# Stationary operands in one piece, two orders of tokens, a column of ones for the denominators, and new schedule constants, in a fused graph-attention and slice-attention layer

## The chip, the cores and the metric

The kernel runs on one core of one Trainium2 chip. The time is device microseconds (us) from launch to end, and a run is one execution. All runs in this document were in the fast state. A profile shows one execution; its engines are PE (TensorE matmuls), PEld (TensorE weight loads, which overlap PE: they are busy for 79% of the span of the kernel before, beside 97% of PE), DVE (VectorE), ACT (ScalarE), POOL (GpSimd) and SP (SyncE, which issues the transfers here).

## The reference, cut to what matters

The input is 32 independent graphs ("batches" below) of 512 tokens with 256 features, all fp32.

```python
x = x + gnn(layernorm(x), adj)        # x: [32, 512, 256]
x = x + ffn(layernorm(x))

def gnn(x, adj):
    out = relu(x @ mlp1_w + mlp1_b)                      # 256 -> 512
    out = elu(gat(out, None, W_fc, a_fc)) + out          # attention over all tokens
    out = relu(out @ mlp2_w + mlp2_b)                    # 512 -> 256
    return relu(elu(gat(out, adj, W_hand, a_hand)) + out)    # masked attention

def gat(inp, mask, W, a):
    h = inp @ W
    e = leaky_relu((h @ a1)[:, :, None] + (h @ a2)[:, None, :])   # masked where adj == 0
    return elu(softmax(e, axis=2) @ h)

def ffn(x):      # 8 heads; the 512 tokens are pooled into 64 slice tokens per head
    w = softmax((x_mid @ W_slice) / temp)                # 512 x 64 weights per head
    token = (w.T @ fx_mid) / (w.sum() + 1e-5)
    token = attention(token)                             # 64 x 64 per head
    return (w @ token) @ W_out
```

## The kernel before

The kernel records all operations of the 32 batches first. A greedy scheduler with a cost model then decides the order of instructions on every engine, and they are issued in that order. The constants that steer it (`TURNS`, `PERIOD`, and shifts `HEAD`, `TAIL` of the first and last three batches) appear to have been tuned for this kernel (b_new_turns below shows another set doing worse in it). The scheduler sees the tiles that each operation reads and writes, its modelled cost, and a key (the time at which its step should have its turn):

```python
TURNS = {"load": -28.1, "norm1": 42.5, "mlp1": 51.4, "h": 105.5, ...}   # key of each step
PERIOD, SPARE = 91.4, 0.00
HEAD, TAIL = (-48.2, -40.6, -1.9), (-3.9, 8.3, 26.1)
...
    def order(self):
        ...                                    # a first schedule of 12 batches gives starts
        shift = dict(enumerate(HEAD)) | {last - i: s for i, s in enumerate(reversed(TAIL))}
        ...
        keys[op] = (age - SAMPLE) * period + turn + shift.get(age, 0.0)
        ...
        return self._schedule(self.ops, keys.get, SPARE)     # greedy, lowest key first

    def emit(self):
        for op in self.order():
            getattr(getattr(self.nc, op.engine), op.method)(*op.args, **op.kwargs)
```

A batch's 512 tokens are loaded so that partition p holds tokens 4p to 4p+3; block t (t = 0..3, `NT` = 4) has token 4p+t at partition p. Where a product needs the features on the partitions, the tile is transposed: VectorE transposes blocks of 32 by 32 into a stage, and five transfers through DRAM move the blocks to their places. For the first and last batch TensorE transposes instead.

```python
    def flip(src, dst):
        nc.vector.transpose(dst, src.rearrange("p (c i) -> p c i", i=Q))     # Q = 32

    def gather(what, stage, dst):
        scr = dram.tile(...)
        for a in range(P // Q):
            nc.sync.dma_start(scr[:, :, a, :].rearrange("c r j -> r c j"), stage[ts(a, Q), :, :])
        nc.sync.dma_start(dst, scr.rearrange("(k c) r a j -> (c r) k (a j)", c=P // Q))

    def every(cols, t):
        return cols[:, t::NT]                  # a step of four words
```

The stage is written with a step (`flip(e, stage[:, :, i::NT])`), so that the columns of the transposed tile are the tokens in natural order. A product whose result shall have block t on its partitions then takes its stationary operand with a step of four words. `matmul(out, stationary, moving)`:

```python
        nc.step = "h"                                     # first attention, W_fc
        ...         nc.tensor.matmul(pm, every(o0T[:, k], t), wfc[:, k, s, :], ...)
        nc.step = "mlp2"
        ...         nc.tensor.matmul(pm, w2[:, k, ts(m)], o1T[:, k, :], ...)
        nc.step = "e"                                     # masked attention
            nc.scalar.activation(e, e, AF.Exp, bias=nmax[:, i:i+1], accum_out=den[:, i:i+1])
            flip(e, stage[:, :, i::NT])
        gather("e", stage, pT)
        nc.vector.reciprocal(rd, den)
        nc.step = "pv2"
        ...         nc.tensor.matmul(pm[:, s, :], every(pT[:, j], i), h[:, j, :D], ...)
        nc.step = "w"                                     # slice weights
        ...         nc.tensor.matmul(pm, every(xnT[:, k], t), weff[:, k, :], ...)
                    flip(wt, stage[:, :, t::NT])
        gather("w", stage, wT)
        nc.step = "tokens"
        ...         nc.tensor.matmul(pm[ts(s, C), p, :], wfx[:, k, ts(2 * p + s, C)],
                                     every(s1T[:, k], p)[:, ts(s, G)], ...)       # 64 wide
        for s in range(2):
            nc.tensor.matmul(pm[ts(s, C)], bfx[:, ts(s, C)], nrow[:, s], ...)     # bias
        nc.step = "out"
        ...         nc.tensor.matmul(po[:, s, :], every(wT[:, p], t), gg[:, p, :], ...)
```

In the groups of the profile these are `mm<-wfc,o0T` (h), `mm<-o1T,w` (mlp2), `mm<-h,p2T` (pv2), `mm<-weff,xn2T` (w), `mm<-xn,w` (sums), `mm<-s1T,wfx` and `mm<-nrow,bfx` (tokens), and `mm<-gg,wT` (out). Every instruction passes through the scheduler's `emit`, so all of them carry the same line number.

Of the kernel before, what the change touches and what calls it, by code (L numbers as in the profile page):

```python
# [16 lines left out]
    "load": -28.1, "norm1": 42.5, "mlp1": 51.4, "h": 105.5, "factors": 105.5, "p": 114.2,  # L17
    "pv": 115.4, "o1": 126.5, "mlp2": 169.7, "h2": 183.7, "e": 190.4, "p2": 190.4,
    "pv2": 203.8, "norm2": 210.0, "w": 285.7, "sums": 288.2, "s1T": 298.5, "tokens": 342.3,
    "att": 351.0, "vo": 351.0, "gg": 361.3, "out": 377.9,  # L20
}
PERIOD, SPARE = 91.4, 0.00

HEAD, TAIL = (-48.2, -40.6, -1.9), (-3.9, 8.3, 26.1)
# [6 lines left out]
P = 128  # L31
# [4 lines left out]
class Recorder:  # L36
# [5 lines left out]
    ISSUE, BEGIN, LAND, BEHIND = 0.45, 1.2, 0.9, 3.0  # L42
# [63 lines left out]
    def _cost(self, op, out, ins):  # L106
# [6 lines left out]
        if op.method == "dma_start":  # L113
            side = next(ap for ap in (out, *ins) if ap.space != bass.MemoryType.DRAM)
            op.moving = out.size() * 4 / (250e3 if side.ap[0][1] <= P // 4 else 320e3)
            return self.ISSUE, 0.0
# [175 lines left out]
def adj_ffn_kernel(  # L292
# [71 lines left out]
    def gather(what, stage, dst):  # L364


        blocks, width = stage.shape[1:]
# [9 lines left out]
    def every(cols, t):  # L377

        return cols[:, t::NT]
# [100 lines left out]
    nc.sync.dma_start(adjt, adj.rearrange("(p t) j -> p t j", p=P))  # L480
    for t in range(NT):
        nc.vector.tensor_scalar(
            mbias[:, t, :].rearrange("p (t q) -> p t q", t=NT),
            adjt[:, t, :].rearrange("p (q t) -> p t q", t=NT), 0.0, None, op0=OP.is_gt,
# [96 lines left out]
    def transpose_features(what, b, src, dst):  # L581

        if by_dma(what, b):
            stage = new(what + "_stage", [P, D // Q, P], tag="stage4")
            for t in range(NT):
                flip(src[:, t, :D], stage[:, :, t::NT])
            gather(what, stage, dst)
            return
        for k in range(KD):
            pt = tr_tile([P, N])  # L590
            for t in range(NT):
                nc.tensor.transpose(pt[:, ts(t)], src[:, t, ts(k)], ident)
            nc.scalar.copy(
                dst[:, k, :].rearrange("p (q t) -> p t q", t=NT),
                pt.rearrange("p (t q) -> p t q", t=NT),
            )
# [13 lines left out]
    def front(b):  # L610
# [8 lines left out]
        transpose_features("xn", b, xn, xnT)  # L619
# [13 lines left out]
        for t in range(NT):  # L633
            for s in range(2):
                pm = mm_tile([P, HH + 1])
                for k in range(KH):
                    nc.tensor.matmul(
                        pm, every(o0T[:, k], t), wfc[:, k, s, :],
                        start=(k == 0), stop=(k == KH - 1),
                    )  # L640
# [48 lines left out]
        for i in range(NT):  # L689
# [11 lines left out]
            if by_dma("u", b):  # L701
                flip(u, stage[:, :, i::NT])
# [4 lines left out]
            nc.vector.tensor_tensor(o1T[:, :, i::NT], pt, o0T[:, :, i::NT], op=OP.add)  # L707
        nc.step = "o1"
        if by_dma("u", b):
            gather("u", stage, o1T)  # L710
            for m in range(KH):
                nc.vector.tensor_tensor(o1T[:, m, :], o1T[:, m, :], o0T[:, m, :], op=OP.add)
        return o1T

    def middle(b, o1T):
# [3 lines left out]
        for m in range(KD):  # L719
            pm = mm_tile([P, N])  # L720
            for k in range(KH):
                nc.tensor.matmul(
                    pm, w2[:, k, ts(m)], o1T[:, k, :], start=(k == 0), stop=(k == KH - 1)
# [4 lines left out]
        for t in range(NT):  # L728
            pm = mm_tile([P, D + 2])
            for k in range(KD):  # L730
                nc.tensor.matmul(
                    pm, every(o2T[:, k], t), wh[:, k, :], start=(k == 0), stop=(k == KD - 1)
# [11 lines left out]
        den = small("den", [P, NT])  # L744
        nmax = small("nmax", [P, NT])
        for i in range(NT):
# [8 lines left out]
            nc.scalar.activation(  # L755
                e, e, AF.Exp, bias=nmax[:, i : i + 1], accum_out=den[:, i : i + 1]
            )
            if by_dma("e", b):
                flip(e, stage[:, :, i::NT])
# [4 lines left out]
            nc.scalar.copy(pT[:, :, i::NT], pt)  # L764
# [3 lines left out]
        rd = small("rd2", [P, NT])  # L768
        nc.vector.reciprocal(rd, den)

        r2 = new("r2", [P, NT, D])
        if by_dma("o2", b):
            stage = new("o2_stage", [P, N // Q, KD * Q], tag="stage4")
            for k in range(KD):
                nc.vector.transpose(
                    stage[:, :, ts(k, Q)].rearrange("p (t c) i -> p t c i", t=NT),
                    o2T[:, k, :].rearrange("p (c i t) -> p t c i", t=NT, i=Q),
                )
            gather("o2", stage, r2)
        else:  # L780
            for t in range(NT):
                pt = tr_tile([P, D])
# [263 lines left out]
```

## Time and profile before

| | before |
|---|---|
| time, median of the first 3 runs | 2926.81 us (2921.08 to 2928.37) |
| profiled span, granted TensorE clock | 2918.5 us, 0.991 |
| TensorE busy | 97% |
| weight loads busy | 79% |
| VectorE busy | 76% |
| ScalarE busy | 36% |

One number does most of the work below. The **period** is the time from the first mlp2 matmul of the 7th batch to that of the 27th, over 20: what one batch costs in the steady middle. It was 87.87 us. The **ends** are the span less 32 periods: filling, draining, and whatever batches near the two ends cost above or below the period. They were 2918.5 - 32 x 87.87 = 106.7 us. The span is then a sum of two things that different parts of the change may move. The prediction shows the views of the kernel before on which it rests.

### The profile page before, as it was taken

How to read it: one execution, taken by the hardware profiler on the slowest of the kernel's cores; microseconds unless marked ns; L12 is line 12 of the kernel's file. 1: busy time of each engine (PE TensorE's matmuls, PEld its weight loads, DVE VectorE, ACT ScalarE, POOL GpSimd, SP SyncE). 2: the span in 40 equal slices, each digit the busy share in tenths (PEclk: the TensorE clock that was granted, in tenths of full speed). 3: DMA queues.
4: the chain of work that ended last, by engine and by line, in shares of the span. 5: the costliest groups of instructions: out<-in, count | busy, mean ns of one | idle time of the engine just before them, and what ended most of it. 6: DMA issues, size and time to landing. Idle time of an engine off the chain costs nothing.

```text
span 2918.5 us, 34260 instructions
## 1 busy us (share of the span) xinstructions
PE 2827.3 (97%) x11981; PEld 2301.0 (79%) x11981; DVE 2231.4 (76%) x4994; ACT 1042.8 (36%) x2058; POOL 125.2 (4%) x233
## 2 busy tenths in 40 slices
PE   8999899999999999999999999999999999999998
PEld 6787668887778887878887878887878877777776
DVE  6567768877778877778877778877778877788774
ACT  3533323333333333333333333333333333333232
POOL 0000000000000000000000000000000000000000
PEclk9999999999999999999999999999999999999998
DMA  5125345454445454445444445444445444444420
GB/s 163 31 72 143 96 128 152 129 147 131 134 139 151 127 148 129 135 135 157 123 145 130 137 137 156 126 144 130 138 137 153 129 140 129 136 138 116 137 73 15
DMA packets 459365, 373.24 MB, mean 128 GB/s; under 512 B 82229, under 2 KB 376761, under 8 KB 459065
## 3 DMA queue, kind: packets, MB, share of 16 engines
q1 hardware_dynamic: 455856, 368.92, 43.8%
q10 hardware_dynamic: 3336, 2.14, 0.2%
q8 instruction: 95, 1.56, 0.2%
q14 instruction: 78, 0.63, 0.1%
HBM read 196.91 MB, written 174.06 MB: 127 GB/s over the span
## 4 chain that ended last, share of the span: by engine, by line
PE 61%; DVE 21%; DMA 11%; SPq 3%; issue 2%; ACT 1%; DVEq 0%; ACTq 0%
PE mm L255 58%; DMA scr<-e_stage 5%; DVE e_stage L255 4%; SPq L255 3%; DMA o1T<-scr 3%; DVE e L255 3%; DVE w L255 3%; DVE w_stage L255 2%; PE tr L255 2%; DVE rs L255 2%; DVE nmax L255 2%; DMA scr<-u_stage 1%; PE sm L255 1%; DVE u L255 1%; DVE mx L255 1%
## 5 line engine op out<-in xcount | busy, mean ns | idle before, releaser
L255 PEld LDWEIGHTS mm<-wfc,o0T 128*128 128x128 f32 x2048 | 491.4, 327 | 19.3 <-PE tr L255 5.5
L255 PE MATMUL mm<-wfc,o0T 128*128 128x257 f32 x2048 | 498.7, 398 | 0.0
L255 PE MATMUL mm<-h,pT 128*128 128x256 f32 (+1 forms) x2048 | 486.8, 379 | 0.0
L255 PEld LDWEIGHTS mm<-h,pT 128*128 128x128 f32 x2048 | 390.2, 191 | 51.9 <-issue 2.8
L255 PE MATMUL mm<-xn,w 128*128 128x257 f32 x1024 | 272.8, 392 | 37.7 <-DVE fm L255 17.4
L255 PE MATMUL mm<-h,p2T 128*128 128x256 f32 x1024 | 301.3, 400 | 0.4 <-DMA p2T<-scr 0.4
L255 PEld LDWEIGHTS mm<-h,p2T 128*128 128x128 f32 x1024 | 266.7, 321 | 9.9 <-DMA p2T<-scr 0.7
L255 PE MATMUL mm<-xnT,w 128*128 128x512 f32 x512 | 258.6, 614 | 3.6 <-ACT xnT L255 3.3
L255 PE MATMUL mm<-gg,wT 128*128 128x256 f32 x1024 | 260.3, 401 | 0.0
L255 PEld LDWEIGHTS mm<-gg,wT 128*128 128x128 f32 x1024 | 251.5, 329 | 11.1 <-ACT gg L255 0.2
L255 PEld LDWEIGHTS mm<-xn,w 128*128 128x128 f32 x1024 | 186.6, 194 | 84.2 <-issue 50.6
L255 PE MATMUL mm<-weff,xn2T 128*128 128x512 f32 x512 | 243.6, 608 | 0.1
L255 ACT COPY h<-mm 128x257 f32<-128x257 f32 (+1 forms) x384 | 141.6, 369 | 279.6 <-PE mm L255 274.8
L255 PE MATMUL mm<-o1T,w 128*128 128x512 f32 x512 | 230.0, 602 | 9.6 <-DVE o1T L255 9.6
L255 DVE TENSOR_TENSOR o1T<-o1T,o0T 128x512 f32<-128x512 f32 x120 | 75.2, 687 | 157.6 <-DMA o1T<-scr 157.6
L255 PEld LDWEIGHTS mm<-o1T,w 128*128 128x128 f32 x512 | 96.0, 191 | 124.7 <-issue 91.6
L255 DVE SCALAR_TENSOR_TENSOR e<-f2b,h,mbias 128x512 f32<-128x512 f32 x128 | 92.4, 743 | 131.0 <-ACT f2b L255 129.0
L255 ACT ACTIVATE u<-mm,rd 128x256 f32<-128x256 f32 x192 | 90.0, 471 | 266.0 <-PE mm L255 159.1
L255 PEld LDWEIGHTS mm<-weff,xn2T 128*128 128x128 f32 x512 | 151.8, 315 | 40.2 <-ACT xn2T L255 1.3
L255 ACT ACTIVATE m<-m 128x512 f32<-128x512 f32 x192 | 118.0, 626 | 154.6 <-DVE m L255 154.1
L255 ACT ACTIVATE e<-e,nmax 128x512 f32<-128x512 f32 x128 | 92.4, 722 | 199.3 <-DVE nmax L255 199.3
L255 DVE STREAM_TRANSPOSE o_stage<-o2T 128x512 f32<-128x512 f32 x60 | 66.5, 1108 | 125.6 <-ACT o2T L255 123.9
(147 smaller groups left out, 4203.9 us busy)
## 6 DMA issues: line engine op xcount, KB each, us to landing
scr<-xn_stage SPq DMA_DIRECT2D x240, 128.0 KB, 2.6
scr<-u_stage SPq DMA_DIRECT2D x120, 256.0 KB, 4.5
o1T<-scr SPq DMA_DIRECT2D x30, 1024.0 KB, 6.1
scr<-e_stage SPq DMA_DIRECT2D x120, 256.0 KB, 4.9
p2T<-scr SPq DMA_DIRECT2D x30, 1024.0 KB, 5.6
scr<-w_stage SPq DMA_DIRECT2D x120, 256.0 KB, 4.1
wT<-scr SPq DMA_DIRECT2D x30, 1024.0 KB, 5.7
xt<-in_x_dram SPq DMA_DIRECT2D x32, 512.0 KB, 4.0
```

Source lines behind the costliest of these rows:

```text
L255: getattr(getattr(self.nc, op.engine), op.method)(*op.args, **op.kwargs)
```

## The change

The intent is that every stationary operand is read in one piece. VectorE then writes its transposes in one piece too. After such a transpose and the gather, column a\*128 + t\*32 + i of the transposed tile is row 32a+i of block t. A contiguous piece of 128 columns is a block in a second order of tokens, and a second transpose leads back to the first order. Most products can live with that. Where the order has to be the old one, either the moving operand is read in swapped runs of 32 words (mlp2, tokens), or ScalarE copies the tile into order (w, xn2). In the masked attention the weights are in one order before their transpose and in the other after it. The denominators that the exponential accumulated would be in the wrong order, so they now come out of the product itself, as a 257th column of ones. The constants of the scheduler were replaced as well.

```diff
-TURNS = {"load": -28.1, "norm1": 42.5, ..., "out": 377.9}
-PERIOD, SPARE = 91.4, 0.00
-HEAD, TAIL = (-48.2, -40.6, -1.9), (-3.9, 8.3, 26.1)
+TURNS = {"load": -182.4, "norm1": -141.0, ..., "out": 181.5}
+PERIOD, SPARE = 88.0, 0.00
+HEAD, TAIL = (-3.1, -0.9, -0.1), (-1.0, -1.3, -1.0)
-    ISSUE, BEGIN, LAND, BEHIND = 0.45, 1.2, 0.9, 3.0        # cost model of a transfer
+    ISSUE, BEGIN, LAND, BEHIND = 0.45, 1.2, 0.9, 2.7
...
-    def every(cols, t):
-        return cols[:, t::NT]
+    def swapped(cols):
+        return cols.rearrange("p (t a i) -> p a t i", t=NT, i=Q)
...
-                flip(src[:, t, :D], stage[:, :, t::NT])
+                flip(src[:, t, :D], stage[:, :, ts(t, Q)])      # u, e, w, s1 likewise
...
-                        pm, every(o0T[:, k], t), wfc[:, k, s, :],
+                        pm, o0T[:, k, ts(t)], wfc[:, k, s, :],  # o2T, pT, xn2T, wT likewise
...
-                    pm, w2[:, k, ts(m)], o1T[:, k, :], ...
+                    pm.rearrange("p (a t i) -> p a t i", t=NT, i=Q), w2[:, k, ts(m)],
+                    swapped(o1T[:, k, :]), ...
...
-            nc.scalar.activation(e, e, AF.Exp, bias=nmax[:, i:i+1], accum_out=den[:, i:i+1])
+            nc.scalar.activation(e, e, AF.Exp, bias=nmax[:, i:i+1])
+        nc.vector.memset(h[:, :, D], 1.0)
-                        pm[:, s, :], every(pT[:, j], i), h[:, j, :D],
+                        pm, pT[:, j, ts(i)], h[:, j, : D + 1],
+                rd = small("rd2", [P, 1])
+                nc.vector.reciprocal(rd, pm[:, D : D + 1])
...
+            raw = new("w_raw", [P, NP, N], tag="w")             # xn2_raw likewise
+            gather("w", stage_w, raw)
+            for p in range(NP):
+                nc.scalar.copy(wT[:, p, :].rearrange(...), swapped(raw[:, p, :]))
...
-                        every(s1T[:, k], p)[:, ts(s, G)],
+                        s1T[:, k, :].rearrange("p (a n i) -> p n a i", n=NP, i=Q)[:, p, ts(s, 2)],
```

Cut out are the first and last batch's additions and copies, the load of `adj` in four pieces, the transposes of o2 (now by VectorE in the first and last batch too), and one transfer rate of the cost model (250e3 to 215e3).

## The prediction

> **What bounds the kernel now.** I read the busy shares first, then one steady batch in the table of windows (columns: PE, PEld, DVE, ACT, POOL busy, granted clock, DMA share, GB/s).
>
> ```profile
> PE 2827.3 (97%) x11981; PEld 2301.0 (79%) x11981; DVE 2231.4 (76%) x4994; ACT 1042.8 (36%) x2058; POOL 125.2 (4%) x233
> ...
> 1737.00:1825.00 88.00, 87.21 (x371) 71.19 (x370) 70.18 (x157) 31.52 (x63) 3.91 (x7) 1.00 0.48 138
> ```
>
> TensorE is busy 97% of the span and 87.2 of 88 us in the middle, at full clock. So the middle is bound by TensorE's own pace, and what a matmul costs there is its start-to-start distance, not its duration, since matmuls overlap. The timeline gives that distance: start of the next row minus start of this one, over the count.
>
> ```profile
> 1737.47 7.12 PE L255 MATMUL mm<-o1T,w 128*128 128x512 f32 x16
> ...
> 1754.67 4.47 PE L255 MATMUL mm<-weff,xn2T 128*128 128x512 f32 x10
> 1758.98 5.28 PE L255 MATMUL mm<-wfc,o0T 128*128 128x257 f32 x22
> ...
> 1767.88 6.23 PE L255 MATMUL mm<-wfc,o0T 128*128 128x257 f32 x26
> 1773.94 2.33 PE L255 MATMUL mm<-xn,w 128*128 128x257 f32 x10
> ...
> 1793.65 10.55 PE L255 MATMUL mm<-h,pT 128*128 128x257 f32 x48
> 1804.04 0.27 PE L255 MATMUL sm<-ident,s 128*4 128x128 f32 x1
> ...
> 1825.21 1.12 PE L255 MATMUL mm<-o1T,w 128*128 128x512 f32 x2
> ```
>
> wfc,o0T: (1773.94 - 1767.88)/26 = 233 ns. h,pT, nearly the same moving width: (1804.04 - 1793.65)/48 = 216 ns. The first takes its stationary operand with a step of four words (columns t, t+4, ...), the second in one piece. The difference is 17 ns. The first and the last row are the same step of two successive batches: a batch takes 87.7 us. 32 of them are 2806 us; the other 112 us of the 2918.5 us span are filling and draining.
>
> The groups show the same in the weight loads:
>
> ```profile
> L255 PEld LDWEIGHTS mm<-wfc,o0T 128*128 128x128 f32 x2048 | 491.4, 327 | 19.3 <-PE tr L255 5.5 <-issue 2.1
> L255 PEld LDWEIGHTS mm<-h,pT 128*128 128x128 f32 x2048 | 390.2, 191 | 51.9 <-issue 2.8 <-DVE pT L255 0.5
> L255 PEld LDWEIGHTS mm<-weff,xn2T 128*128 128x128 f32 x512 | 151.8, 315 | 40.2 <-ACT xn2T L255 1.3 <-issue 0.5 <-PE tr L255 0.2
> L255 DVE STREAM_TRANSPOSE e_stage<-e 128x512 f32<-128x512 f32 x120 | 133.9, 1116 | 5.4 <-DMA scr<-w_stage 2.8 <-ACT e L255 2.4
> L255 DVE TENSOR_TENSOR o1T<-o1T,o0T 128x512 f32<-128x512 f32 x120 | 75.2, 687 | 157.6 <-DMA o1T<-scr 157.6
> L255 ACT COPY acb<-tr 128x512 f32<-128x512 f32 x64 | 37.3, 585 | 43.8 <-PE tr L255 43.8
> L255 ACT COPY wT<-tr 128x512 f32<-128x512 f32 x8 | 8.8, 1101 | 10.8 <-PE tr L255 10.8
> ```
>
> A stepped load takes 327 ns against 191 ns. Behind a 512-wide matmul (weff,xn2T) it doesn't matter: (1758.98 - 1754.67)/10 = 431 ns, the width's own pace.
>
> [...] 17 ns of the 136 ns show in the pace of a 257-wide matmul, none in a 512-wide one. [...] The e_stage transposes write with that step; 1116 ns is 1.6 times the 687 ns of an ordinary 512-wide operation here. [...] the one group with a contiguous output (o_stage, 1108 ns) reads with a step.
>
> **The change part by part.**
> *Stationary operands in one piece.* The stepped matmuls narrower than 512 are wfc,o0T 2048, gg,wT 1024, h,p2T 1024 and wh,o2T 512: 4608. At 17 ns each that is 78 us, nearly all on the bound engine, so on the path. weff,xn2T gives nothing. mlp2 and the token products now stream their moving operand in runs of 32 words; I expect 429 to 431 ns as now. Gain 78 us (2.4 us a batch).
> *Column of ones.* h,p2T grows from 256 to 257 columns: 1024 x 0.84 ns (216/257) = 0.9 us more on TensorE. ScalarE loses 128 accumulator reads of 187 ns, 24 us; VectorE gets 128 reciprocals from PSUM (161 ns, as those of the first attention) for 32 of 140 ns, and 32 memsets of 62 ns, about 18 us more. Neither is the bound.
> *Transposes with contiguous output.* All DVE transposes sum to 133.9 (e) + 131.6 (u) + 131.1 (w) + 131.4 (both xn) + 77.1 (s) + 66.5 (o) = 672 us. If the step was what made them slow, the 420 of 512 go to about 690 ns and the 360 of 256 from 640 to about 420 ns: 441 us, so 230 us less VectorE. That bears only where TensorE waits for VectorE. In a steady batch I added what each start-to-start distance has over the median of its form: 2.7 us, of which 1.3 us in the sums, waiting for the softmax weights. The chain of waits shows how:
>
> ```profile
> 1773.10 1.12 DVE w_stage L255
> 1774.22 0.47 DVE rs L255
> 1774.69 1.02 DVE w_stage L255
> 1775.71 0.53 DVE rs L255 x2
> 1776.24 0.60 DVE w L255
> 1776.84 0.11 DVE rs L255
> 1776.99 0.67 PE mm L255 x2
> ```
>
> Two transposes stand in the FIFO just ahead of the last weights. Four e and two w transposes, each 0.35 us shorter in pace, would take the wait away: up to 32 x 1.3 = 42 us. I count a third, 13 us, because whether the transpose gets faster is unproven and the new order leaves less room: from the first weff matmul to the second sums matmul there are about 20 us of TensorE work in the new order of instructions, about 25 in the old.
> *Reordering copies.* w and xn2 now land in a raw tile and ScalarE copies it: 30 x 6 copies of about 0.59 us (acb) = 106 us, bringing ScalarE to about 1110 us, 39%. Beside other work, unless the in-order ScalarE stands waiting for the gather.
> *First and last batch.* Their 36 stepped copies and additions of 1.1 us (28 on ScalarE, 8 on VectorE) lose about 0.5 us each: 18 us, of which I put 4 us on the path. The token products may gain too; I count nothing.
> Sum: 2926.8 - 78 + 1 - 13 - 4 = 2833 us.
>
> **Rivals.**
> *A. A wait takes the place of the pace.* The w gather can start only after the sums have released w, since the raw tile has its buffer, and four copies that wait for it stand in ScalarE's queue between two exponentials of the attention; the raw xn2 copies stand ahead of the o2T relu. A gather takes 5 to 6 us to land, behind four writes of 4 to 5 us. If it is late by 1 us a batch, 32 us of the gain go: about 2865. Against it: in TensorE's order the product that needs wT comes over 40 us after the sums.
> *B. The transposes become fast and the waits in the sums go.* 78 + 42 + some at the ends: about 2795. For it: the equal 1.1 us of every stepped operation on two engines. Against: o_stage.
> *C. Filling and draining.* The schedule is a new one. From the order, 89 us of TensorE work are left after the last batch's first mlp2 matmul, against 78 before, where 110 us passed in fact; and the second batch starts mlp2 after 118 us of work instead of 128. This can move the ends by 20 us either way.
> *D. Nothing: the loads were hidden anyway.* Then 2920. The 17 ns are measured in the pace itself, so I give this little.
>
> **Range and chances.** 78 us is the firm part and alone gives 2849. A and C push up, B and C down by 20 to 40 us: 2790 to 2880. A gain of over 2% needs under 2868 us, 19 us above the firm part; that takes A or C at full size with the transposes unchanged. Chances 0.85 faster, 0.13 within 2%, 0.02 slower.
>
> **What would show it right or wrong.** Right: LDWEIGHTS near 191 ns in wfc,o0T, gg,wT, h,p2T and wh,o2T, their distance near 216 ns, a batch of about 84.9 us, TensorE still at 97%. Transposes at 0.69 and 0.42 us, VectorE near 2020 us, no wait of the sums for rs: rival B at work. Wrong: TensorE idle ahead of the o2T products or after pv2 with ScalarE waiting for w_raw or xn_raw (A); a moving operand in runs of 32 that costs more than 431 ns; distances still at 233 ns.

## The result, and the profile after

| | before | after |
|---|---|---|
| time, median (4 runs each, all fast) | 2925.9 us | 2728.3 us (2727.1 to 2731.7) |
| ratio of fast runs (95%) | 1 | 0.9328 (0.9312 to 0.9345) |
| profiled span | 2918.5 us | 2725.3 us |
| granted clock | 0.991 | 0.997 |
| period | 87.87 us | 83.10 us |
| ends (span less 32 periods) | 106.7 us | 66.1 us |

A ratio is always the mean time of one kernel's fast runs over that of the other's of the same rounds, so it is not quite the ratio of the medians. Below, "us against after" is a difference of medians; runs of the kernel before stood beside every call, with medians between 2920.0 and 2925.9 us, so calls can be compared within some 6 us.

The gain was nearly 200 us, twice what was predicted, and the time lies below the range of 2790 to 2880 us. Of the 193 us of span, 32 x 4.77 = 153 us came from the period and 40 us from the ends.

First come the busy shares and the chain that ended last of the kernel after:

```profile
PE 2667.5 (98%) x11965; PEld 1988.7 (73%) x11965; DVE 2057.3 (75%) x5126; ACT 1117.4 (41%) x2102; POOL 124.6 (5%) x233
...
PE 73%; DMA 13%; DVE 9%; SPq 2%; issue 2%; ACT 1%; ACTq 0%; POOL 0%; DVEq 0%; POOLq 0%
```

The chain of the kernel before stood like this:

```profile
PE 61%; DVE 21%; DMA 11%; SPq 3%; issue 2%; ACT 1%; DVEq 0%; ACTq 0%
```

TensorE stays the bound, as predicted. VectorE's share of the chain fell from 21% to 9%: less of the time now runs through VectorE.

Next are the groups of the kernel after, by form (out<-in, partitions x elements, count | busy us, mean ns | idle before, and what ended it):

```profile
L255 PEld LDWEIGHTS mm<-wfc,o0T 128*128 128x128 f32 x2048 | 386.2, 189 | 131.1 <-issue 84.9 <-PE tr L255 0.2
...
L255 PE MATMUL mm<-xn,w 128*128 128x257 f32 x1024 | 244.7, 382 | 4.8 <-DVE w L255 4.8
...
L255 DVE STREAM_TRANSPOSE e_stage<-e 128x512 f32<-128x512 f32 x120 | 84.2, 702 | 0.8 <-ACT e L255 0.8
...
L255 DVE STREAM_TRANSPOSE o_stage<-o2T 128x512 f32<-128x512 f32 x64 | 45.6, 712 | 171.0 <-ACT o2T L255 171.0
```

The rows of the kernel before that the prediction does not show are these:

```profile
L255 PE MATMUL mm<-xn,w 128*128 128x257 f32 x1024 | 272.8, 392 | 37.7 <-DVE fm L255 17.4 <-DVE w L255 9.5 <-DVE rs L255 6.0
...
L255 DVE STREAM_TRANSPOSE o_stage<-o2T 128x512 f32<-128x512 f32 x60 | 66.5, 1108 | 125.6 <-ACT o2T L255 123.9 <-issue 1.7
```

The weight loads fell from 327 to 189 ns. The transposes fell from 1.1 to 0.7 us, and o_stage did so too, in which the step had been in the input and not in the output. The sums (mm<-xn,w) used to wait 37.7 us for VectorE and now wait 4.8 us.

The steady batch of the kernel after, in the timeline of TensorE (start us, us from the first start to the last end, count, and in brackets the idle time before it and its releaser), has:

```profile
1545.61 7.13 PE L255 MATMUL mm<-o1T,w 128*128 128x512 f32 x16 [0.40 <-DVE o1T L255]
...
1574.20 4.07 PE L255 MATMUL mm<-wfc,o0T 128*128 128x257 f32 x18
1578.10 0.59 PE L255 MATMUL mm<-xn,w 128*128 128x257 f32 x2
...
1603.19 0.30 PE L255 MATMUL mm<-s1T,wfx 128*64 128x64 f32 x2 [0.41 <-DMA s1T<-scr]
...
1606.81 0.69 PE L255 MATMUL mm<-s1T,wfx 128*64 128x64 f32 x16
1607.43 2.00 PE L255 MATMUL mm<-h,pT 128*128 128x256 f32 x8
...
1609.96 0.65 PE L255 MATMUL mm<-nrow,bfx 4*64 4x256 f32 x4
1610.54 1.13 PE L255 MATMUL mm<-xnT,w 128*128 128x512 f32 x2
...
1628.88 1.55 PE L255 MATMUL mm<-o1T,w 128*128 128x512 f32 x3 [0.34 <-DVE o1T L255]
```

wfc,o0T: (1578.10 - 1574.20)/18 = 217 ns, the distance that only h,pT had before. From the first to the last row the batch takes 83.3 us. The token products, s1T,wfx, take (1607.43 - 1606.81)/16 = 39 ns each. The two bias products, nrow,bfx, take 1610.54 - 1609.96 = 0.58 us together. (Each fp32 matmul of the program shows as two records on TensorE in these traces, 128 of nrow,bfx for the two bias products of 32 batches, which is why two bias products are four records. The times of a matmul in this document and in the prediction are those of a record.) The same stretch of the kernel before looks like this:

```profile
1804.24 2.07 PE L255 MATMUL mm<-s1T,wfx 128*64 128x64 f32 x32
1806.24 2.84 PE L255 MATMUL mm<-xnT,w 128*128 128x512 f32 x6
1809.02 0.64 PE L255 MATMUL mm<-nrow,bfx 4*64 4x256 f32 x2
1809.59 1.13 PE L255 MATMUL mm<-xnT,w 128*128 128x512 f32 x2
1810.64 0.64 PE L255 MATMUL mm<-nrow,bfx 4*64 4x256 f32 x2
1811.21 1.13 PE L255 MATMUL mm<-xnT,w 128*128 128x512 f32 x2
```

Here a token product took (1806.24 - 1804.24)/32 = 62.5 ns (a record, as above), and the two bias products took 0.57 + 0.57 = 1.14 us, with an mlp1 matmul between them. Neither was in the prediction. Each bias product writes 64 of the 128 output partitions. Next to each other the two run at once: in the trace of the kernel after their records start in pairs, 6 to 7 ns apart, and in that of the kernel before 267 ns lie between the two records of the second one. So the pair costs what one cost, 0.58 us against 0.57.

The ends can be seen in the busy time of stretches. The first row of each fence is from the second batch's first mlp2 matmul to the seventh's. The second row is a piece of the steady middle (in the fence of before some 5.0 batches, in that of after likewise). The third row is from the 27th batch's first mlp2 matmul to the last batch's. Before:

```profile
150.10:595.20 445.10, 423.04 (x1781) 342.69 (x1779) 328.23 (x730) 157.10 (x313) 17.68 (x33) 0.98 0.43 123
1747.00:2186.00 439.00, 434.97 (x1846) 355.27 (x1846) 349.49 (x780) 158.05 (x317) 19.58 (x35) 1.00 0.48 138
2352.70:2808.70 456.00, 440.51 (x1870) 362.79 (x1871) 349.09 (x765) 157.48 (x313) 17.78 (x33) 0.99 0.43 124
```

After:

```profile
139.30:546.00 406.70, 401.89 (x1818) 301.43 (x1818) 306.36 (x760) 169.52 (x320) 18.50 (x33) 1.00 0.51 135
1545.00:1960.00 415.00, 412.17 (x1841) 307.05 (x1840) 321.44 (x802) 172.92 (x325) 18.73 (x35) 1.00 0.55 146
2207.90:2611.30 403.40, 400.31 (x1811) 299.74 (x1812) 311.94 (x773) 168.84 (x317) 18.57 (x33) 1.00 0.51 136
```

The first two numbers after the stretch are its length and TensorE's busy time. Five batches at the period are 439.4 us before and 415.5 us after. Before, the stretch on the way in is 5.8 us longer than that and the one on the way out 16.7 us longer; after, they are 8.8 and 12.1 us shorter. That is 14.6 + 28.8 = 43 us. What lies outside them makes up the rest: the second batch comes 6 us earlier (periods taken off), and the time behind the last batch's first mlp2 matmul is 9 us longer (likewise). Most of the 43 us is idle time of TensorE: 22.1 us on the way in (445.10 - 423.04) and 15.5 us on the way out before, against 4.0 in the middle; 4.8, 3.1 and 2.8 us after. Less the middle's own, the idle time fell by 16.1 + 11.2 = 27 us. Most of the rest goes with the granted clock, the third number from the end of each row: 0.98 and 0.99 in the two stretches before, 1.00 after. If TensorE sets the pace there, that is some 0.02 x 445 + 0.01 x 456 = 13 us, an estimate. So it is not the filling and draining themselves that changed, but the batches next to them.

### The profile page after: what moved, and what is told of

Same layout as the page of the kernel before. It is cut to its first block, busy times and chain, and to the rows that moved or that the text cites. A ratio compares the mean times of both kernels' runs of the same rounds, so it can differ in the third digit from the quotient of the medians.

```text
span 2725.3 us, 34426 instructions
## 1 busy us (share of the span) xinstructions
PE 2667.5 (98%) x11965; PEld 1988.7 (73%) x11965; DVE 2057.3 (75%) x5126; ACT 1117.4 (41%) x2102; POOL 124.6 (5%) x233
## 4 chain that ended last, share of the span: by engine, by line
PE 73%; DMA 13%; DVE 9%; SPq 2%; issue 2%; ACT 1%; ACTq 0%; POOL 0%; DVEq 0%; POOLq 0%
PE mm L255 70%; DMA o1T<-scr 4%; DMA scr<-s_stage 3%; SPq L255 2%; PE tr L255 2%; DMA s1T<-scr 2%; DVE u L255 1%; DMA w_raw<-scr 1%; DVE u_stage L255 1%; DVE xn L255 1%; DMA scr<-u_stage 1%; DVE xn_stage L255 1%; PE sm L255 1%; DVE vo L255 1%; DVE o1T L255 0%
## 5 line engine op out<-in xcount | busy, mean ns | idle before, releaser
L255 PEld LDWEIGHTS mm<-wfc,o0T 128*128 128x128 f32 x2048 | 386.2, 189 | 131.1 <-issue 84.9
L255 PE MATMUL mm<-h,pT 128*128 128x257 f32 (+1 forms) x2048 | 467.3, 382 | 0.4 <-ACT u L255 0.2
L255 DVE TENSOR_TENSOR x<-mm,x 128x512 f32<-128x512 f32 x64 | 44.2, 691 | 292.8 <-PE mm L255 292.8
L255 PE MATMUL mm<-xn,w 128*128 128x257 f32 x1024 | 244.7, 382 | 4.8 <-DVE w L255 4.8
L255 PE MATMUL mm<-h,p2T 128*128 128x257 f32 x1024 | 242.0, 380 | 0.7 <-ACT p2T L255 0.7
L255 PEld LDWEIGHTS mm<-gg,wT 128*128 128x128 f32 x1024 | 189.6, 190 | 35.1 <-issue 6.5
L255 PEld LDWEIGHTS mm<-h,p2T 128*128 128x128 f32 x1024 | 187.0, 190 | 28.2 <-ACT p2T L255 0.9
L255 PEld LDWEIGHTS mm<-xnT,w 128*128 128x128 f32 x512 | 92.6, 191 | 68.8 <-issue 50.9
L255 ACT ACTIVATE m<-m,neg 128x512 f32<-128x512 f32 x192 | 138.0, 719 | 3.6
L255 DVE SCALAR_TENSOR_TENSOR u<-m,u 128x512 f32<-128x512 f32 x192 | 131.6, 686 | 9.1 <-ACT m L255 7.7
```

## The experiments

Fourteen kernels ran, and two things about them matter. Because the scheduler's order depends on what it sees, an edit to one operation can reorder everything. So in several experiments the order was worked out with the original operation, and only then was one argument replaced:

```python
    def instead(self, place, ap):      # what runs; the order was worked out with the other one
        args = list(self.ops[-1].args)
        args[place] = ap
        self.ops[-1].args = tuple(args)
```

The orders of all engines in those kernels were compared with the original's and are the same. The second thing: some of these kernels compute something wrong on purpose, because a step in one place then meets data in the other order; instructions, sizes and traffic are the same.

| kernel | median us | ratio to before (95%) | period us | ends us |
|---|---|---|---|---|
| before | 2925.9 | 1 | 87.87 | 106.7 |
| after | 2728.3 | 0.9328 (0.9312 to 0.9345) | 83.10 | 66.1 |
| a_step_stationary | 2799.6 | 0.9573 (0.9559 to 0.9587) | 85.13 | 70.8 |
| a_step_transposes | 2839.1 | 0.9710 (0.9695 to 0.9724) | 86.60 | 66.5 |
| b_whole_transposes | 2862.3 | 0.9788 (0.9768 to 0.9808) | 86.15 | 104.5 |
| b_new_turns | 2954.6 | 1.0102 (1.0080 to 1.0123) | 90.07 | 69.3 |
| a_step_tokens | 2749.5 | 0.9415 (0.9399 to 0.9430) | 83.83 | 67.3 |
| a_nrow_apart | 2768.3 | 0.9477 (0.9459 to 0.9494) | 84.63 | 57.8 |
| a_nrow_apart2 | 2769.6 | 0.9473 (0.9450 to 0.9496) | 84.70 | 60.5 |
| a_no_ones | 2821.9 | 0.9670 (0.9651 to 0.9689) | 86.71 | 46.0 |
| a_old_turns | 2836.3 | 0.9712 (0.9696 to 0.9727) | 85.72 | 90.9 |
| b_whole_new_turns | 2925.1 | 1.0004 (0.9980 to 1.0028) | 89.02 | 70.7 |
| a_accum_back | 2734.6 | 0.9349 (0.9326 to 0.9372) | 83.12 | 74.2 |
| v_s1T_first | 2712.7 | 0.9282 (0.9259 to 0.9304) | 82.67 | 71.2 |
| a_old_ends | 2819.1 | 0.9662 (0.9646 to 0.9679) | 85.36 | 81.3 |
| b_new_ends | 2906.5 | 0.9956 (0.9941 to 0.9971) | 87.81 | 93.8 |

Names with a start from the kernel after, names with b from the kernel before.

### a_step_stationary: the step back into the stationary operands (wrong on purpose)

```diff
                     nc.tensor.matmul(pm, o0T[:, k, ts(t)], wfc[:, k, s, :], ...)
+                    nc.instead(1, o0T[:, k, t::NT])          # o2T, pT, xnT, wT likewise
```

> The changed kernel in its own order of instructions, but the stationary operands of wfc,o0T, h,p2T, wh,o2T, weff,xn2T and gg,wT are read with a step of four words again; everything else as changed (the result is wrong on purpose). Theory: 4608 matmuls go back from 216 to 233 ns, 78 us, so about 2806 us and LDWEIGHTS near 327 ns. Rival (the pace was hardly worth anything, the gain came from waits and the order): under 2745 us. Rival (the loads were also behind the rest, for instance the token products): over 2840 us.

It took 2799.6 us: 71 us against after, and 2.03 us more a batch. The load group shows that this is the old load again:

```profile
L261 PEld LDWEIGHTS mm<-wfc,o0T 128*128 128x128 f32 x2048 | 510.9, 324 | 44.9 <-issue 0.5 <-PE tr L261 0.2
```

The prediction's 78 us (2.44 us a batch) stands with a small error. This part explains 71 us of nearly 200, and no more. Some of the lost pace hides in waits that the kernel after has anyway: in the 20 middle batches TensorE's idle time is 1.7 us here and 14.0 us in the kernel after.

### a_step_transposes: the step back into VectorE's transposes (wrong on purpose)

```diff
-    def flip(src, dst):
+    def flip(src, dst, step):
         nc.vector.transpose(dst, src.rearrange("p (c i) -> p c i", i=Q))
+        nc.instead(0, step)                                  # stage[:, :, t::NT]
...
+            nc.instead(1, o2T[:, k, :].rearrange("p (c i t) -> p t c i", t=NT, i=Q))
```

> The changed kernel in its own order, but every VectorE transpose writes (o_stage reads) with a step of four words, as before (wrong result on purpose). Theory: transposes return from 0.70 and 0.42 us to 1.1 and 0.64 us, 230 us more VectorE, and the 80 us of TensorE waits that went come back for the most part: 2780 to 2810 us. Rival (the new order of instructions took the waits away, not the faster transposes): within 15 us of 2728 us.

It took 2839.1 us, above the forecast: 111 us against after and 3.5 us more a batch. The step alone makes the transposes slow, and TensorE then waits longer, among others for the softmax weights. The groups of this kernel show both:

```profile
L261 PE MATMUL mm<-xn,w 128*128 128x257 f32 x1024 | 252.7, 386 | 34.3 <-DVE w L261 32.2 <-DVE sc L261 1.2 <-DVE fm L261 0.5
...
L261 DVE STREAM_TRANSPOSE e_stage<-e 128x512 f32<-128x512 f32 x120 | 133.1, 1109 | 0.9 <-ACT e L261 0.8
```

The first row has the sums waiting 32.2 us for w, against 4.8 us in the kernel after, and the second the transposes at 1109 ns. Over the trace, the waits for s1T also rose (from 15.3 to 23.9 us), and those for fm on VectorE from 0.7 to 11.5 us. The transposes had been worth a third of 42 us to the prediction.

### b_whole_transposes: only the transposes changed, in the old order (wrong on purpose)

```diff
-    def flip(src, dst):
+    def flip(src, dst, whole):
         nc.vector.transpose(dst, src.rearrange("p (c i) -> p c i", i=Q))
+        nc.instead(0, whole)                                 # stage[:, :, ts(t, Q)]
...
+                nc.instead(1, o2T[:, k, :].rearrange("p (t c i) -> p t c i", t=NT, i=Q))
```

> The kernel before in its own order, with transposes that write and read in one piece (wrong result on purpose) and nothing else of the change. Theory that the transposes end the waits: 40 to 80 us faster than before, 2845 to 2885 us. Rival (the new order did it): within 15 us of 2926 us.

It took 2862.3 us, 61 us less than the kernel before of the same call (2923.2). The period fell by 1.72 us and the ends by 2 us. The transposes are at 704 ns, and what the sums' distances have over the median of their form fell from 58 to 23 us over the whole trace (in the 20 middle batches from 1.3 us a batch to nothing):

```profile
L261 PE MATMUL mm<-xn,w 128*128 128x257 f32 x1024 | 261.1, 388 | 13.5 <-DVE w L261 6.7 <-DVE rs L261 4.3 <-DVE ex L261 1.4
...
L261 DVE STREAM_TRANSPOSE e_stage<-e 128x512 f32<-128x512 f32 x120 | 84.5, 704 | 7.2 <-ACT e L261 4.2 <-DMA scr<-w_stage 2.3
```

So the transposes are worth 61 us in the old order of instructions and 111 us in the new one. That the new order leaves less time between the softmax weights and their use, as the prediction counted, fits this; it was not tested by itself.

### b_new_turns: the kernel before with the schedule constants of after (correct)

```diff
-TURNS = {"load": -28.1, ...};  PERIOD = 91.4;  HEAD, TAIL = (-48.2, ...), (-3.9, ...)
+TURNS = {"load": -182.4, ...};  PERIOD = 88.0;  HEAD, TAIL = (-3.1, ...), (-1.0, ...)
-    BEHIND = 3.0;  250e3
+    BEHIND = 2.7;  215e3
```

> The kernel before with only the schedule constants of the change (TURNS, PERIOD, HEAD, TAIL and the two DMA constants). If the new order took the waits away: 40 to 80 us faster than before. If the new order needs the faster transposes: no faster than before, perhaps slower by some per cent.

It took 2954.6 us, 1% slower than before: the ends fell from 106.7 to 69.3 us, but the period rose from 87.87 to 90.07 us. The ends belong to the constants for the most part, then, and not to the layout (a_old_turns below has 90.9 us with the new layout). The period does not, because the greedy scheduler sorted this instruction set anew and put the steps of the token chain behind each other without enough other work between them. TensorE waits 22.2 us ahead of wvo,tokbd, 30.5 us ahead of the transposes of attbd and 14.9 us ahead of tok,wqk here. Of the 44 us that the 20 middle batches take longer than before, 28 are idle time of TensorE; the granted clock is also lower there, 0.987 against 1.000.

### a_step_tokens: the step back into the token products' moving operand

```diff
                     nc.tensor.matmul(pm[ts(s, C), p, :].rearrange(...), wfx[...], s1T[...], ...)
+                    nc.instead(0, pm[ts(s, C), p, :])
+                    nc.instead(2, s1T[:, k, p::NP][:, ts(s, G)])
```

> The changed kernel in its own order, but the token products read s1T with a step of four words as moving operand, as before (wrong result on purpose). Theory: the step is what made them slow, 66.2 us of start-to-start distance in the trace before against 46.7 us now, so about 19 us more, 2745 to 2750 us. Rival (the new place in the order made them faster): within 5 us of 2728 us, and the distances stay at 46 ns.

It took 2749.5 us, 21 us against after. It mixes up token columns on purpose; the comparison with the reference nevertheless let it pass. In the timeline of TensorE:

```profile
1616.01 1.13 PE L261 MATMUL mm<-s1T,wfx 128*64 128x64 f32 x16
1617.07 2.00 PE L261 MATMUL mm<-h,pT 128*128 128x256 f32 x8
```

Sixteen of them take 1.06 us, 66 ns each, against 0.62 us in the kernel after. The 64-wide fp32 matmul is slowed by a step in its moving operand, from 39 to 66 ns a record. This was the smallest change in the diff, and the prediction counted nothing for it.

### a_nrow_apart: an mlp1 matmul back between the two bias products (correct)

```diff
     def emit(self):
-        for op in self.order():
+        done = self.order()
+        at = [i for i, op in enumerate(done) if op.engine == "tensor"]
+        nrow = [n for n, i in enumerate(at) if "nrow" in done[i].args[2].tensor.name]
+        for a, b in zip(nrow[::2], nrow[1::2]):
+            c = b + 1
+            if b == a + 1 and done[at[c]].step == "mlp1":
+                done.insert(at[b], done.pop(at[c]))   # the next matmul goes between the pair
+        for op in done:
```

A first version that moved the second bias product back instead was refused by the simulator's memory check before any run: another product then read the accumulator before its group was closed. The version shown moves the other matmul.

> The changed kernel with one matmul of the next batch's mlp1 moved between the two nrow,bfx products of a batch, as they stood in the order before; correct result. Theory: [...] 4 x 267 ns instead of 2 x 267, about 0.5 us a batch on TensorE, 13 to 16 us in all, about 2742 us. Rival (TensorE finds other slack there): under 5 us.

It took 2768.3 us, 40 us against after; the period rose by 1.53 us and the ends gave back 8 us. The timeline of TensorE shows the edit and what it uncovers:

```profile
1631.61 0.64 PE L263 MATMUL mm<-nrow,bfx 4*64 4x256 f32 x2
1632.77 0.70 PE L263 MATMUL mm<-tok,wqk 128*128 128x256 f32 x2 [0.52 <-DVE tok L263]
```

Start-to-start, the bias products' sum over the trace rose from 20.8 to 52.9 us. Without a wait, 128 records that do not run at once take 128 x 267 ns = 34 us, so some 13 us are the pair that no longer runs at once. The other 19 us are the wait for tok on VectorE behind the second of them, which the moved mlp1 matmul had covered.

### a_nrow_apart2: the same, with the cover restored (correct)

```diff
+                # as in a_nrow_apart; then the next mlp1 matmul is pulled ahead of tok,wqk
```

> As a_nrow_apart, but with a second mlp1 matmul between the second nrow,bfx product and the product with wqk, as in the order before, so that the copy of the tokens on VectorE again has cover; correct result. Theory: [...] 2740 to 2750 us. Rival (separation itself costs 40 us): 2760 us or more.

It took 2769.6 us, so the forecast of 2740 to 2750 us missed. It put some 15 of the 40 us of a_nrow_apart down to the pair that no longer runs at once, and the rest to the missing cover. The timeline of TensorE shows why:

```profile
1550.87 0.64 PE L266 MATMUL mm<-nrow,bfx 4*64 4x256 f32 x2
1551.44 1.12 PE L266 MATMUL mm<-xnT,w 128*128 128x512 f32 x2
1552.49 0.64 PE L266 MATMUL mm<-nrow,bfx 4*64 4x256 f32 x2
...
1554.96 1.56 PE L266 MATMUL mm<-wvo,tokbd 128*128 128x256 f32 x6 [0.34 <-POOL tokbd L266]
```

The wait for tok is gone, but the matmul that was put ahead is missing after tok,wqk, and TensorE waits for GpSimd's tokbd there. The sums of the distances over the trace account for most of the 41 us: the bias products rose from 20.8 to 37.7 us, tok,wqk from 15.7 to 27.9, wvo,tokbd from 58.5 to 67.1 and mlp1 from 225.3 to 230.6, 43 us together. So the cover was moved and not restored, and no run has the pair apart with full cover. The saving of the pair side by side is read from its own distances: about 14 us (34.4 us in the kernel before, 20.8 after).

### a_no_ones: the accumulated denominators back (not meant to be wrong, and it was)

```diff
-            nc.scalar.activation(e, e, AF.Exp, bias=nmax[:, i:i+1])
+            nc.scalar.activation(e, e, AF.Exp, bias=nmax[:, i:i+1], accum_out=den[:, i:i+1])
-        nc.vector.memset(h[:, :, D], 1.0)
+        nc.vector.reciprocal(rd2, den)
-                pm = mm_tile([P, D + 1])
+                pm = mm_tile([P, D])                         # and 256-wide products
```

> The changed kernel without the column of ones: denominators of the masked attention from the accumulator of the exponential and one reciprocal of four columns, h,p2T 256 wide; the order is worked out anew. Theory: the column of ones is worth little, within 15 us of 2728 us either way (0.9 us less TensorE, 24 us more ScalarE, 18 us less VectorE). Rival (it took a wait out of the e chain): 2745 us or more.

The result was wrong (relative error 2.10). The denominators stand in the order of e's rows, and the product's rows are in the other order. The column of ones is not a saving, then, but a part without which the two orders don't work. The time of 2821.9 us says little about it: the order was worked out anew for the changed instruction set, and waits in the token chain are back. The longest is that of tok,wqk (us in total, times, longest), beside 8.5 us ahead of wvo,tokbd:

```profile
PE mm L255 <- DVE tok L255: 43.8, 28, 2.2
```

Waiting is not all. The 20 middle batches take 72 us longer than in the kernel after: TensorE's idle time rose by 31 us, but its busy time rose by 42 us for the same 7361 records. The granted clock there is 0.97 against 1.00, and the median distance of wvo,tokbd is 426 ns against 216. What lowered the clock was not tested.

### a_accum_back: only the accumulator back, in the order of after (correct)

```diff
             nc.scalar.activation(e, e, AF.Exp, bias=nmax[:, i:i+1])
+            nc.ops[-1].kwargs["accum_out"] = den[:, i:i+1]
```

> The changed kernel in its own order, with the accumulator output of the masked exponentials added again (nobody reads it); correct result. Adds 128 reads of 187 ns to ScalarE, 24 us. Theory: beside other work, 2728 to 2733 us. Rival (ScalarE is on the path of the e chain): 2740 us or more.

It took 2734.6 us with an interval of the ratio (0.9326 to 0.9372) that covers 0.9328. The medians differ by 6 us, no more than calls differ by, and the period did not move (83.12 against 83.10). So it is not shown that the 128 accumulator reads which the change took from ScalarE gave anything.

### a_old_turns: the kernel after with the schedule constants of before (correct)

The diff is that of b_new_turns with the signs exchanged.

> The changed kernel with the schedule constants of before (TURNS, PERIOD, HEAD, TAIL, the two DMA constants). With the transposes alone the kernel before reached 2862 us; minus 71 for the stationary operands and 19 for the tokens that is 2772 us. If the new order is worth the remaining 44 us: 2760 to 2790 us. If the order is worth nothing and the column of ones or the copies did it: within 10 us of 2728 us.

It took 2836.3 us, so both forecasts missed. The ends rose to 90.9 us and the period to 85.72 us. It is still 84 us faster than the kernel before of the same call (2920.7): that much the layout gives with the old constants. With b_new_turns this says that layout and constants belong together: each set of constants gives its better period with the instruction set that it came with.

### b_whole_new_turns: the kernel before with whole transposes and the new constants (wrong on purpose)

The diff is that of b_whole_transposes and that of b_new_turns together.

> The kernel before with transposes in one piece (wrong result on purpose) and the new schedule constants, nothing else. Of the four combinations of the two this one is missing. If the new order pays once the transposes are fast: below 2862 us by the 35 us that it saves at the two ends, about 2825 us. If the new order only suits the new data layout as a whole: 2862 us or more.

It took 2925.1 us, as long as the kernel before. It tested whether the new order needs nothing but the fast transposes. It doesn't: the period of 89.02 us is 1.05 us better than b_new_turns and still above the 87.87 us of before. What is left are the waits of the token chain in this order, which are those of b_new_turns to 0.1 us (30.5, 22.2 and 14.9 us).

### v_s1T_first: the gather of w behind that of s1T (correct; faster than both kernels)

In the kernel after, the first two token products wait for s1T, as its timeline above shows. The transfers that SyncE issues are in this order (start us, us in the queue, transfer, count):

```profile
1591.90 0.38 SPq L255 DMA_DIRECT2D w_raw<-scr  x1
1592.34 0.55 SPq L255 DMA_DIRECT2D scr<-s_stage  x1
1599.41 0.38 SPq L255 DMA_DIRECT2D s1T<-scr  x1
```

The large w_raw gather, whose product gg,wT starts only at 1622.77, some 30 us later, goes out just ahead of the last of the four writes on which s1T depends. The chain of the kernel after shows what that write then takes, 6.99 us:

```profile
1592.34 6.99 DMA scr<-s_stage
...
1599.41 3.64 DMA s1T<-scr
1603.05 0.14 issue
1603.19 2.83 PE mm L255 x12
```

The edit moves the gather behind s1T's, and the four copies that wait for it behind in ScalarE's queue:

```diff
     def emit(self):
+        for each batch:
+            the gather w_raw<-scr goes right behind the gather s1T<-scr on SyncE
+            the four copies wT<-w_raw go just ahead of the first exponential of attbd on ScalarE
```

> An attempt to beat the changed kernel: after the schedule is worked out, the w gather is issued behind the s1T gather instead of ahead of its last write, and its four copies stand just ahead of the attention's exponential, where ScalarE idled for 3 us; correct result. TensorE waited 0.4 to 0.9 us a batch for s1T: if that goes, 10 to 25 us faster, 2705 to 2718 us. If another wait takes its place: 2728 us or slower.

It took 2712.7 us and is correct. That is 16 us less than after; the intervals of the two ratios to before (0.9259 to 0.9304 and 0.9312 to 0.9345) don't touch, though the two did not run in the same rounds. In its timeline of SyncE the order is:

```profile
1584.30 1.82 SPq L274 DMA_DIRECT2D scr<-s_stage  x4
1588.30 0.38 SPq L274 DMA_DIRECT2D s1T<-scr  x1
1588.86 0.38 SPq L274 DMA_DIRECT2D w_raw<-scr  x1
```

From the first write's issue to that of the s1T gather it is now 4.0 us instead of 1599.41 - 1590.36 = 9.05 us (the first three writes of the kernel after are issued from 1590.36 on). The wait of the token products for s1T fell from 15.3 to 7.2 us over the trace, and the copies no longer wait for w_raw at all (35.7 to 0.0 us). The two edits were made together. But the profiled spans differ by 8.7 us (2725.3 and 2716.6), and the wait for s1T fell by 8.1 us of that, so the transfers' order is the likelier cause of the two.

### a_old_ends: only HEAD and TAIL of before, in the kernel after (correct)

This run and the next one were made beyond the twelve, because the 40 us of the ends were still open: are they the shifts of the first and last batches, or the turns?

```diff
-HEAD, TAIL = (-3.1, -0.9, -0.1), (-1.0, -1.3, -1.0)
+HEAD, TAIL = (-48.2, -40.6, -1.9), (-3.9, 8.3, 26.1)
```

> The changed kernel with HEAD and TAIL (the shifts of the first three and last three batches) of before, its TURNS unchanged; correct result. If HEAD and TAIL saved the 40 us at the ends: about 2765 us, with the steady period still 83.1 us. If the turns did it: within 15 us of 2728 us.

It took 2819.1 us. The ends rose by 15 us to 81.3, not to 106. What was not meant is that the period rose too, by 2.26 us, although the shifts touch only six batches. The timeline of a middle batch shows where:

```profile
1574.52 0.65 PE L255 MATMUL mm<-nrow,bfx 4*64 4x256 f32 x4
1575.69 0.70 PE L255 MATMUL mm<-tok,wqk 128*128 128x256 f32 x2 [0.53 <-DVE tok L255]
1577.27 1.13 PE L255 MATMUL mm<-wvo,tokbd 128*128 128x256 f32 x4 [0.88 <-POOL tokbd L255]
...
1581.37 0.44 PE L255 MATMUL tr<-ident,attbd 128*128 128x128 f32 x2 [1.21 <-ACT attbd L255]
```

The greedy order of the middle depends on where the first batches put it. With these shifts it falls into an order in which the short steps of the token chain follow each other, and TensorE waits for tok, tokbd and attbd in turn: 0.53 + 0.88 + 1.21 us in this batch. (Over the 20 middle batches, 45 us longer than in the kernel after, the idle time is 38 us more.)

### b_new_ends: only HEAD and TAIL of after, in the kernel before (correct)

The diff is that of a_old_ends with the signs exchanged.

> The kernel before with HEAD and TAIL of the change, its TURNS unchanged; correct result. If HEAD and TAIL saved the 40 us at the ends: about 2885 us. If the turns did it, or the shifts suit only their own turns: 2920 us or more.

It took 2906.5 us. The ends fell by 13 us to 93.8 and the period stayed (87.81). So the shifts give about 13 to 15 of the 40 us, and the other 25 or so are left for the turns and the other constants, which set how deep the batches overlap. That is a difference and not a run of its own.

## Why the prediction was wrong

The direction and the mechanism of its main term were right. The size was not: three terms were missing or far too small. Period and ends say it best.

| term | predicted | measured |
|---|---|---|
| stationary operands | -78 us | -71 us (2.03 us a batch) |
| transposes in one piece | -13 us | -61 us in the old order (1.72 us a batch) |
| token products | 0 | -21 us (0.73 us a batch) |
| the two bias products | not seen | about -14 us (13.6/32 = 0.43 us a batch) |
| column of ones, accumulator, copies | +1 us | accumulator alone: within 6 us; the others not measured |
| ends | -4 us | -40 us |

The first four terms make 2.03 + 1.72 + 0.73 + 0.43 = 4.91 us a batch, where 4.77 were measured. That they come so close is in part chance, since they are taken from two orders: taken out of the kernel after instead of added to the one before, the transposes alone are worth 3.5 us a batch. The start-to-start distances of the 20 middle batches can be added without that choice. In us a batch, from before to after: wfc,o0T, gg,wT, h,p2T and wh,o2T -2.24, the sums -1.32, the token products -0.54, the bias products -0.55, mlp1 and weff,xn2T, whose matmuls now have fewer waits among them, -0.87, and h,pT +0.92, much of it new waits for s1T behind it. That makes -4.60 of -4.77.

**Stationary operands in one piece.** The mechanism was right. The distance of wfc,o0T fell from 233 to 217 ns and its loads from 327 to 189 ns, as written down. The term came out 7 us high.

**Transposes.** This is the step that failed first: "I count a third, 13 us, because whether the transpose gets faster is unproven and the new order leaves less room". The prediction's reasoning for doubt was that o_stage, whose output was contiguous, took 1108 ns; but its input had the step. A step on either side makes the transpose slow (1108 ns with it in the input, 1116 ns in the output), and without any it takes 702 to 712 ns. The step costs (1108 - 712)/512 = 0.77 ns per column in the input and (1116 - 702)/512 = 0.81 ns in the output. ScalarE's copies, in the groups that the prediction shows, had a cost of a step in the output, too: 1101 ns with it (wT) and 585 ns without (acb). Without a step, the transpose takes about as long as an ordinary 512-wide operation: 702 ns beside 687 ns. VectorE came down to 2057 us, near the 2020 of the prediction. The bound on what that could give, "up to 32 x 1.3 = 42 us", was right for the sums: in the middle of b_whole_transposes their 1.3 us a batch went in full (35 us over the trace, with the ends). It left out the other waits for VectorE. Ahead of mlp2, which waits for the sum o1T, the excess over the trace fell from 17 to 4 us in that run; the remaining 13 or so of its 61 us are not taken apart. Rival B was the right one, and it too was too small.

**Token products.** "The token products may gain too; I count nothing" failed: 21 us. The trace before had the number to ask about: a 64-wide product took 62.5 ns, at a quarter of the width of wfc,o0T more than a quarter of its time (233/4 = 58 ns), and they start two at a time, 7 to 14 ns apart. A step in the stationary operand was recognised as a cost, and one in a narrow moving operand was not asked about. For the 512-wide mlp2, whose moving operand the change reads in runs of 32 words, the expected pace without loss was right: the median distance is 429 ns in both kernels (the groups' mean durations are 602 and 597 ns).

**Bias products.** Not in the prediction at all. It is not the layout that makes them faster, but the new order of instructions, which happens to put them side by side (so does b_new_turns, with the old layout; in a_old_turns they stand apart). For the prediction this was luck.

**Ends.** The prediction gave them 4 us, and in rival C at most 20 us. It counted the work ahead of the second batch's and behind the last batch's first mlp2 matmul, and that count was not bad: 10 us less work on the way in came out as 139.3 instead of 150.1 us, and 11 us more on the way out as 114.0 instead of 109.8. What it did not count are the batches between the ends and the middle. TensorE's stalls there, 22.1 and 15.5 us in five batches each, were in the profile, in the busy time of stretches, and so was the lower granted clock of these stretches (0.98 and 0.99); the prediction looked only at a steady batch. The runs show that they belong to the constants for the most part (ends of 69 and 71 us in b_new_turns and b_whole_new_turns, with the old layout), 13 to 15 us of it to the shifts of the first and last batches.

**Rival A.** ScalarE's copies stayed beside other work (41% busy, against the 39% predicted), and the copy of w waited 35.7 us for its gather. But the gather itself delayed another transfer, s1T's last write (6.99 us, where the median of these writes is 2.7 us from issue to landing); v_s1T_first, which moved both gather and copies, gained about 16 us. The prediction looked for this wait in the engine's queue; it was in the transfers'.

**Is the gain the layout's, or the schedule's?** Both. The layout with the old constants gained 84 us (a_old_turns). The new constants without the layout gained nothing (2925 and 2955 us), but on the layout they gave the other 108 us. Whatever made the scheduler sort the kernel after anew (a_no_ones, a_old_turns, a_old_ends) landed at 2819 to 2836 us, some 100 us above it and near the prediction of 2833. That nearness is luck: in a_old_turns TensorE waits 60.8 us ahead of the sums, more than the 37.7 us of the kernel before, and the ends fell by 16 us, where the prediction had less waiting and 4 us. What stays open is why exactly one set of constants gives the good order of the token chain, how the 25 us of the turns split between depth and order, what lowered the clock in some orders, and what the column of ones costs alone, for which no correct kernel with the two orders can be built without it.

## What to carry to other kernels

Look for steps in every operand of every engine at once, stationary, moving, input and output of a transpose, and compare each group's duration with that of an ordinary operation of its size (here 1116 ns for a transpose beside 687 ns); a group that is slower than its width is a question that the blind estimate has to answer. When TensorE is bound in the middle, read the stretches next to both ends separately, since their stalls need not be those of a steady batch (here 22.1 and 15.5 us in five batches, against 4.0 us in the middle), and compare the granted clock of the stretches too. With a greedy scheduler, freeze the order when one part is tested: otherwise the experiment measures the new order and not the part.
